# A two-block graph network: the first block's accumulators in other PSUM banks

## The chip, the cores and the metric

The kernel runs on one core of a Trainium2 chip. The metric is the device time of one execution in microseconds (us), here the median of three runs. The kernel before takes 2522.91 us (2522.33 to 2523.05).

## The reference

There are 16 graphs (`B`), each with 1024 nodes (`N`), 128 features per node and a dense 1024 x 1024 adjacency matrix, all in float32. Two residual blocks follow each other; both use the same matrix, and each ends with a layer norm over the features:

```python
# first block
degree = adj.sum(axis=-1)[:, :, None]
sum_neighbors = einsum('bid,bij->bjd', x, adj) / degree
x = layernorm(x + relu(concat([x, sum_neighbors]) @ W.T + b))
# second block: four layers; layers 2 and 3 also see earlier layers' outputs
def layer(nodes):
    src_agg = einsum('bjv,bij->biv', nodes @ ws + bs, l2norm(adj, 2))
    dst_agg = einsum('bjv,bji->biv', nodes @ wd + bd, l2norm(adj, 1))
    return tanh(concat([src_agg, nodes @ wn + bn, dst_agg]) @ wu + bu)
x = layernorm(x + layer(layer(layer(layer(x)))))
```

So each graph needs one product with its matrix in the first block, and in each of the four layers one with the column-scaled matrix and one with the row-scaled, transposed one.

## The kernel before

**Tiling.** A graph's matrix lies in SBUF as `a`: 128 partitions by 8 rows of blocks by 1024 columns. Node columns are handled in two halves of 512 (`half(h)`)[...]. Results are kept feature by node. The layers' weights are folded: `messages` (L493) makes, by eight or more products per bank `pt`, the two messages of each node, and VectorE evicts them with a bias (L506). `aggregate` (L557) multiplies them with the matrices.

**Strassen-like products.** `aggregate` splits both matrices into quarters, so that some products serve twice. The partial products M1 to M4 stand in four PSUM tiles `A`, `Bk`, `Ck` and `Dk` (three in layer 0), and two more, `Z0` and `Z1`, gather what goes into one output half alone. The upper and the lower half of the PSUM partitions are filled by two lists of products that run as pairs on the two halves of the array (L690). At fixed steps of that list, `events` read the partial products out: `m1_read`, `m4_read` and `m3_half` on ScalarE (L588 to L593, L636), `m2_read` (L596), a sum (L663) and `m3_read` (L600) on VectorE, and then `second_half`, which adds `Z1` (L604), sums (L605) and applies tanh on ScalarE (L703). `Z0` is added after the last product (L692).

**Banks.** [...]`ps_p` holds two, one for each tag p0 and p1, which `product(name, h)` gives out: `Z0` and `Z1` of every layer, and `pa` of the first block. `ps_t` holds four that rotate, under one tag: the message banks `pt`, the partial products, and `pw` of the first block (`product(name)` without a number). `ps_s` holds two for small things. A tile that is asked for gets the bank that has been given back longest, and its first product waits for the last reader of what stood there.

**Order.** The order on TensorE, VectorE, ScalarE and GpSimd is that of the program text. The main loop goes over the graphs `b`. One step of it does layers 0 to 3 of graph `b`; in between it prepares graph `n = b + 1`, by functions that `aggregate` calls at given steps of its list (`hooks`):
- in layer 0, `load(n)` issues the transfers of the next matrix `a2`; in layer 1, `sums` (L245 to L252) takes its row and column sums, on all three engines
- around layer 2, `inverses` forms the norms, and `factor_row` sends them through DRAM into a row on all partitions, `cinv`. With it `scale_columns` (L336) scales `a2` in place: 16 instructions on VectorE, the first eight for half 1 of the columns (steps 12 and 15), four for half 0 at step 19 and four at step 25, with `second_half` between these last two groups
- after layer 2, `factor_row` fetches `dinv`, into the buffer that `cinv` had, and `first_gnn` (L420) does the first block of graph `n`: for half 1 and then half 0, sixteen products (8 rows by two halves of the array) into `pa`, then VectorE multiplies by `dinv` into `agT` (L429); between the halves VectorE also combines two quarters of the matrix (L481). Then `first_weights` multiplies `x` and `agT` with the weights, in `pw`, and ScalarE applies ReLU
- in layer 3 the layer norm of graph `n` and its transposed rows follow.

The very first graph is prepared ahead of the loop by other code, so `first_gnn` runs 15 times.

Of the kernel before, what the change touches and what calls it, by code (L numbers as in the profile page):

```python
# [23 lines left out]
def adj_resnorm_kernel(ctx: ExitStack, tc: tile.TileContext, x, adj, w0, b0, layers, out):  # L24
# [46 lines left out]
    def blocks(ap):  # L71

        return ap.rearrange("p (k g c) -> p g k c", g=G, c=C)
# [5 lines left out]
    def half(h):  # L79
        return slice(h * HW, (h + 1) * HW)  # L80
# [95 lines left out]
    def by_halves(out, x, y, start=True, stop=True):  # L176

        for s in (slice(V, P), slice(V)):
            nc.tensor.matmul(out[s], x[:, s], y, start=start, stop=stop)  # L179

    def product(name, i=None):
        if i is None:
            return ps_t.tile([P, HW], F32, tag="pt", name=name)
        return ps_p.tile([P, HW], F32, tag=f"p{i}", name=name)
# [235 lines left out]
    def first_gnn(b, xn, xT, a, dinv):  # L420

        agT = one.tile([P, N], F32, tag="acc", name=f"agT{b}")
        yT = one.tile([P, N], F32, tag="x", name=f"yT{b}")
        for h in (1, 0):
            s = half(h)
            pa = product(f"pa0_{b}_{h}", h)
            for i in range(NB):
                by_halves(pa, xn[:, i], a[:, i, s], i == 0, i == NB - 1)
            nc.vector.tensor_mul(agT[:, s], pa, dinv[:, s])  # L429
            if h == 1:  # L430
                combine_1(quarters(a))
        for h in (1, 0):
            first_weights(b, h, xT, agT, yT)
        return yT
# [34 lines left out]
    def quarters(a):  # L469
        return {(j, h): a[:, j * NJ:(j + 1) * NJ, half(h)] for j in range(2) for h in range(NH)}  # L470

    def quarters_t(at):
        return {(j, h): at[h][:, j * NJ:(j + 1) * NJ] for j in range(2) for h in range(NH)}
# [5 lines left out]
    def combine_1(y):  # L479

        nc.vector.tensor_sub(y[0, 1], y[0, 1], y[0, 0])  # L481
# [75 lines left out]
    def aggregate(b, l, feats, msgs, a, at, T, Q, fT, etag, hooks={}, pieces=1):  # L557


        w = wown[l]  # L560
        n = len(feats)
        X, S = msgs
        Y = {DST: quarters(a), SRC: quarters_t(at)}
        TT = {DST: T, SRC: Q}
        low, high = slice(0, V), slice(V, P)
        Z0, Z1 = (product(f"z{h}_{l}_{b}", h) for h in range(NH))
        A, Bk, Ck = (product(f"m{i}_{l}_{b}") for i in range(3))
        e0 = one.tile([P, HW], F32, tag="e0", name=f"e0_{l}_{b}")
        e12 = one.tile([P, 2, HW], F32, tag=etag, name=f"e12_{l}_{b}")
        e1, e2 = e12[:, 0], e12[:, 1]  # L570

        def own(v, h):
            return [(w[:, c, v * V:(v + 1) * V], blocks(f[:, half(h)])) for f, c in feats]

        def src(v, h, j):
            return (X[v, j // NJ][:, j % NJ, SRC], at[h][:, j])

        def prod(name, part):
            y, t = Y[part], TT[part]
            x, y = {"M1": lambda: (X[0, 0], y[0, 0]), "M2": lambda: (S[2], t[2]), "M3": lambda: (S[3], t[3]),  # L580
                    "M4": lambda: (S[1], y[0, 1]), "Z11": lambda: (X[0, 1], y[1, 0]),
                    "Z12": lambda: (S[4], y[1, 1]), "Z21": lambda: (X[1, 1], t[4])}[name]()
            return [(x[:, k, part], y[:, k]) for k in range(NJ)]

        def m1_read():
            nc.scalar.copy(e0[high], A[high])  # L588
            nc.scalar.copy(e0[low], A[high])

        def m4_read():
            nc.scalar.copy(e2[high], Ck[low])
            nc.scalar.copy(e2[low], Ck[low])  # L593

        def m2_read():
            nc.vector.tensor_add(e0[high], e0[high], Bk[high])  # L596
            nc.scalar.copy(e1[low], e0[high])

        def m3_read():
            nc.vector.tensor_add(e0[high], e0[high], A[high])  # L600
            nc.scalar.copy(e1[high], e0[high])

        def second_half():
            nc.vector.tensor_add(e2, e2, Z1)  # L604
            nc.vector.tensor_add(e1, e1, e2)  # L605
            squash(l, 1, e1, fT)


        if l == 0:
            upper = [  # L610
                (Z1, True, own(1, 1)), (Z0, True, own(1, 0)),
                (Z1, False, [src(1, 1, j) for j in range(2, NB)]),
                (A, True, prod("M1", DST)), (Bk, True, prod("M2", DST)), (A, True, prod("M3", DST)),
                (Z0, False, prod("Z21", DST) + [src(1, 0, j) for j in range(NB)]),
            ]
            lower = [
                (Z1, True, own(0, 1)), (Z0, True, own(0, 0)),
                (Z1, False, [(S[2][:, j, SRC], at[1][:, j]) for j in range(2)] + [src(0, 1, j) for j in range(2, NB)]),
                (Ck, True, prod("M4", DST) + [src(1, 1, j) for j in range(2)]),
                (Z1, False, prod("Z12", DST)),  # L620
                (Z0, False, prod("Z11", DST) + [src(0, 0, j) for j in range(NB)]),
            ]
            def m4_and_m2_read():
                m4_read()
                m2_read()

            def m3_and_second_half():
                m3_read()
                second_half()

            events = {10: m1_read, 14: m4_and_m2_read, 18: m3_and_second_half}
        else:
            Dk = product(f"m3_{l}_{b}")

            def m3_half():
                nc.scalar.copy(e1[high], Dk[low])  # L636


            first_of_lower = [(Ck, True, prod("M4", DST) + prod("M4", SRC)), (Dk, True, prod("M3", DST))]
            reads_of_lower = [m4_read, m3_half]  # L640
            if l < NL - 1:
                first_of_lower.reverse()
                reads_of_lower.reverse()
            upper = [
                (Z1, True, own(1, 1)), (Z0, True, own(1, 0)),
                (A, True, prod("M1", DST) + prod("M1", SRC)), (Bk, True, prod("M2", DST) + prod("M2", SRC)),
                (A, True, prod("M3", SRC)),
                (Z0, False, prod("Z21", SRC) + prod("Z21", DST)),
            ]
            lower = [  # L650
                (Z1, True, own(0, 1)), (Z0, True, own(0, 0)),
                *first_of_lower,
                (Z1, False, prod("Z12", SRC) + prod("Z12", DST)),
                (Z0, False, prod("Z11", SRC) + prod("Z11", DST)),
            ]

            def first_reads():
                m1_read()
                reads_of_lower[0]()

            def m2_and_half_of_m3():
                m2_read()
                nc.vector.tensor_add(e0[high], e0[high], e1[high])  # L663

            def last_reads():
                m3_read()
                second_half()

            events = {8: first_reads, 12: reads_of_lower[1], 16: m2_and_half_of_m3, 20: last_reads}

        def steps(groups, rows):
            flat = []
            for m, (acc, first, mms) in enumerate(groups):
                later = [g[1] for g in groups[m + 1:] if g[0] is acc]
                last = not later or later[0]
                for i, (x, y) in enumerate(mms):
                    flat.append((acc[rows], x, y, first and i == 0, last and i == len(mms) - 1))
            return flat

        up, lo = steps(upper, high), steps(lower, low)  # L680
        assert len(up) == len(lo)
        for i, pair in enumerate(zip(up, lo)):
            if i - 2 * n in events:
                events[i - 2 * n]()
            if i in hooks:
                hooks[i]()
            for o, x, y, start, stop in pair:
                if len(y.shape) == 4:
                    o = nodes(o)
                nc.tensor.matmul(o, x, y, start=start, stop=stop)  # L690
        if pieces == 1:
            nc.vector.tensor_add(e0, e0, Z0)  # L692
            squash(l, 0, e0, fT)
        else:
            width = HW // pieces
            for i in range(0, HW, width):
                nc.vector.tensor_add(e0[:, i:i + width], e0[:, i:i + width], Z0[:, i:i + width])
                nc.scalar.activation(fT[:, i:i + width], e0[:, i:i + width], AF.Tanh, bias=bout[l])
# [83 lines left out]
    pa = [product(f"pa0_0_{h}", h) for h in range(NH)]  # L782
# [386 lines left out]
    b = B - 1  # L1169
# [48 lines left out]
```

## Time and profile before

| | before |
|---|---|
| time, median of 3 | 2522.91 us |
| span of the profiled run | 2517.5 us, granted clock 0.999 |
| instructions of the profiled run | 30270 |
| DMA | 219.63 MB, 87 GB/s in the mean |
| `pa` products (L179) | 960 records, 209.3 us busy |
| layer products (L690) | fourteen groups at 592 to 602 ns each |
| scaling (L336) on VectorE | 250, 683 ns in the median |
| rows `dinv`, issue to landing | 4.5 / 5.0 / 5.8 us, least, median, most |

A float32 product appears in the records as two matmuls, each with its own weight load. Two matmuls of a pair on the two halves of the array start nearly together. In the timeline each row gives the start in us, the length in us, the engine, the line, the operation, the tile written and the tiles read, the shapes and the number of records; brackets hold the idle time of that engine just before, and who ended it. PEld is the weight load of TensorE, SPq the queue that issues transfers. One step of the main loop takes some 154 us (`pa` starts at 305.44, 460.91 and 615.47 us).

### The profile page before, as it was taken

How to read it: one execution, taken by the hardware profiler on the slowest of the kernel's cores; microseconds unless marked ns; L12 is line 12 of the kernel's file. 1: busy time of each engine (PE TensorE's matmuls, PEld its weight loads, DVE VectorE, ACT ScalarE, POOL GpSimd, SP SyncE). 2: the span in 40 equal slices, each digit the busy share in tenths (PEclk: the TensorE clock that was granted, in tenths of full speed). 3: DMA queues.
4: the chain of work that ended last, by engine and by line, in shares of the span. 5: the costliest groups of instructions: out<-in, count | busy, mean ns of one | idle time of the engine just before them, and what ended most of it. 6: DMA issues, size and time to landing. Idle time of an engine off the chain costs nothing.

```text
span 2517.5 us, 30270 instructions
## 1 busy us (share of the span) xinstructions
PE 2487.2 (99%) x11693; PEld 1051.9 (42%) x11693; DVE 1661.8 (66%) x2030; ACT 836.3 (33%) x1553; POOL 519.8 (21%) x217
## 2 busy tenths in 40 slices
PE   8999999999999999999999999999999999999998
PEld 4443344433444344443434434334443344433444
DVE  5858667585665757667576675766758567585643
ACT  5414333142331423324143251432414333142311
POOL 5401204012040221302113030130301203112000
PEclk9999999999999999999999999999999999999999
DMA  9417244171543615436163351635417255271410
GB/s 207 93 45 149 54 97 103 50 143 41 101 101 69 128 34 105 103 65 126 35 125 83 83 108 46 130 67 101 95 44 147 52 97 104 49 143 42 92 24 9
DMA packets 358735, 219.63 MB, mean 87 GB/s; under 512 B 148928, under 2 KB 329408, under 8 KB 358592
## 3 DMA queue, kind: packets, MB, share of 16 engines
q1 hardware_dynamic: 357184, 213.51, 41.6%
q0 software_dynamic: 1408, 4.20, 0.7%
q8 instruction: 92, 1.51, 0.3%
q14 instruction: 51, 0.42, 0.1%
HBM read 199.17 MB, written 18.46 MB: 86 GB/s over the span
## 4 chain that ended last, share of the span: by engine, by line
PE 59%; DVE 12%; DMA 9%; SPq 7%; ACT 4%; POOL 4%; issue 2%; DVEq 0%; POOLq 0%; ACTq 0%
PE m L690 22%; PE z L690 16%; PE pt L503 10%; PE pa L179 8%; SPq L231 7%; DMA a<-in_adj_dram 4%; DVE a L336 3%; DMA cinv<-dr 2%; POOL acc L252 2%; PE pw L179 2%; DMA out_dram<-y 2%; DVE e L663 2%; POOL inv L298 1%; ACT sq L248 1%; DMA dr<-invt 1%
## 5 line engine op out<-in xcount | busy, mean ns | idle before, releaser
L378 POOL TENSOR_TENSOR rs<-ve,mhalf 128x32 f32<-128x32 f32 x30 | 162.8, 5427 | 1377.5 <-DVE ve L376 1377.5
L690 PE MATMUL m<-T,S 128*64 128x512 f32 x1008 | 395.8, 593 | 0.0
L690 PE MATMUL z<-at,t 128*64 128x512 f32 x1224 | 383.7, 592 | 0.0
L690 PE MATMUL m<-a,t 128*64 128x512 f32 x1008 | 366.7, 594 | 0.0
L690 PE MATMUL m<-Q,S 128*64 128x512 f32 x768 | 339.2, 593 | 0.0
L690 PE MATMUL m<-at,t 128*64 128x512 f32 x828 | 311.2, 592 | 0.0
L506 DVE TENSOR_TENSOR t<-pt,wm 128x512 f32<-128x512 f32 x256 | 175.2, 689 | 168.5 <-PE pt L503 168.3
L252 POOL TENSOR_TENSOR acc<-acc,sq 128x1024 f32<-128x1024 f32 x90 | 220.5, 2450 | 141.5 <-ACT sq L248 137.8
L690 PE MATMUL z<-a,S 128*64 128x512 f32 x504 | 228.3, 593 | 0.0
L690 PE MATMUL z<-a,t 128*64 128x512 f32 x504 | 226.8, 592 | 0.0
L690 PE MATMUL z<-T,t 128*64 128x512 f32 x504 | 226.8, 592 | 0.0
L336 DVE TENSOR_TENSOR a<-a,cinv 128x512 f32<-128x512 f32 x250 | 157.6, 696 | 95.8 <-DMA cinv<-dr 91.9
L179 PE MATMUL pa<-a,xn 128*64 128x512 f32 x960 | 209.3, 594 | 10.2 <-DVE e L604 10.2
L457 ACT ACTIVATE a<-a,rinv 128x256 f32<-128x256 f32 x480 | 198.2, 495 | 53.4 <-DMA a<-in_adj_dram 43.1
L503 PE MATMUL pt<-wm,f1T 128*128 128x256 f32 x768 | 213.7, 383 | 0.1
L690 PE MATMUL z<-at,S 128*64 128x512 f32 x444 | 202.6, 593 | 0.0
L690 PEld LDWEIGHTS m<-Q,S 128*64 128x64 f32 x768 | 104.1, 137 | 206.8 <-issue 206.3
L588 ACT COPY e<-m 64x512 f32<-64x512 f32 x63 | 36.6, 581 | 449.1 <-PE m L690 448.7
L690 PEld LDWEIGHTS m<-T,S 128*64 128x64 f32 x1008 | 117.8, 137 | 159.8 <-issue 158.1
L690 PE MATMUL z<-Q,t 128*64 128x512 f32 x384 | 172.6, 592 | 0.0
L690 PEld LDWEIGHTS z<-at,t 128*64 128x64 f32 x1224 | 120.7, 137 | 121.1 <-issue 111.4
L690 PEld LDWEIGHTS m<-a,t 128*64 128x64 f32 x1008 | 110.0, 137 | 125.9 <-issue 120.1
(197 smaller groups left out, 3775.5 us busy)
## 6 DMA issues: line engine op xcount, KB each, us to landing
a<-in_adj_dram SPq DMA_DIRECT2D x120, 512.0 KB, 12.5
a<-in_adj_dram SPq DMA_DIRECT2D x480, 128.0 KB, 4.1
xn<-in_x_dram SPq DMA_DIRECT2D x128, 64.0 KB, 2.0
wm<-wsave SPq DMA_DIRECT2D x16, 512.0 KB, 3.8
wm<-wsave SPq DMA_DIRECT2D x31, 256.0 KB, 2.9
xs<-in_x_dram SPq DMA_DIRECT2D x60, 128.0 KB, 3.6
cinv<-dr SPq DMA_DIRECT2D x30, 256.0 KB, 5.0
dinv<-dr SPq DMA_DIRECT2D x30, 256.0 KB, 5.0
```

The source lines that it names most:

```text
L179: nc.tensor.matmul(out[s], x[:, s], y, start=start, stop=stop)
L231: nc.sync.dma_start(ov[g, :, ks], ys[g * C:(g + 1) * C, ks])
L248: nc.scalar.activation(sq, a[:, i, :], AF.Square, accum_out=cols[:, i:i + 1])
L252: nc.gpsimd.tensor_add(acc, acc, sq)
L336: engine.tensor_mul(a[:, i, s], a[:, i, s], cinv[:, s])
L378: nc.gpsimd.tensor_tensor(rstd, ve, mhalf[:, :n], ALU.pow)
L457: nc.scalar.activation(st[:, k], st[:, k], AF.Copy, scale=rinv[:, q * QB + k:q * QB + k + 1])
L503: nc.tensor.matmul(pt[:, q], f[:, i * P:(i + 1) * P], wm[:, 1 + c], start=(k == 0), stop=(k == nch - 1))
L506: nc.vector.tensor_add(t[j][:, o:o + 2].rearrange("p k a v c -> p k (a v c)"), pt, wm[:, 0][:, None, :].to_broadcast([P, 2, 2 * P]))
L588: nc.scalar.copy(e0[high], A[high])
L663: nc.vector.tensor_add(e0[high], e0[high], e1[high])
L690: nc.tensor.matmul(o, x, y, start=start, stop=stop)
```

## The change

`first_gnn` no longer takes the banks of `Z0` and `Z1` for `pa`, but two of the rotating pool, so that its first products need not wait until the layer before has been read out of `Z1` and `Z0`. In return, `aggregate` asks for the banks of the partial products in another order: `Ck` (M4) and `Dk` (M3) first, since they are read first, then `A` and `Bk`. So the banks that come back to `pa` are those that are given back early. The order of the products, of the reads and of the transfers stays as it was.

```diff
@@ first_gnn
         for h in (1, 0):
             s = half(h)
-            pa = product(f"pa0_{b}_{h}", h)
+            pa = product(f"pa0_{b}_{h}")
             for i in range(NB):
                 by_halves(pa, xn[:, i], a[:, i, s], i == 0, i == NB - 1)
@@ aggregate
         Z0, Z1 = (product(f"z{h}_{l}_{b}", h) for h in range(NH))
-        A, Bk, Ck = (product(f"m{i}_{l}_{b}") for i in range(3))
+
+        Ck = product(f"m4_{l}_{b}")
+        Dk = product(f"m3_{l}_{b}") if l else None
+        A, Bk = (product(f"m{i}_{l}_{b}") for i in (1, 2))
@@ aggregate, layers 1 to 3
-            Dk = product(f"m3_{l}_{b}")
-
             def m3_half():
```

## The prediction

> **What bounds the kernel now.** The page first, its busy times: TensorE is the only full engine, at the full granted clock, so only time in which TensorE stands still, or does more, can move the end.
>
> ```profile
> PE 2487.2 (99%) x11693; PEld 1051.9 (42%) x11693; DVE 1661.8 (66%) x2030; ACT 836.3 (33%) x1553; POOL 519.8 (21%) x217
> PEclk9999999999999999999999999999999999999999
> ```
>
> Then the waits of TensorE alone (columns: who waited, for whom, us in total, times, longest). The reader is to see that one row holds almost half of all its idle time (10.2 of about 23 us), that the others come once or three times, and that the row is the accumulator which this change moves.
>
> ```profile
> engine line waited for: us in total, times, longest us
> PE pa L179 <- DVE e L604: 10.2, 14, 2.0
> PE w0tr L770 <- POOL inv L759: 6.3, 1, 6.3
> ```
>
> Then the timeline of one such place, all engines (start, length). It is the longest of the fifteen, in the graph step that ends layer 2 near 458 us.
>
> ```profile
> 458.36 0.59 PE L690 MATMUL z<-T,t 128*64 128x512 f32 x1
> 458.37 0.59 PE L690 MATMUL z<-a,t 128*64 128x512 f32 x1
> 458.65 0.69 DVE L663 TENSOR_TENSOR e<-e,e 64x512 f32<-64x512 f32 x1 [0.68 <-ACT e L597]
> 459.45 0.69 DVE L600 TENSOR_TENSOR e<-e,m 64x512 f32<-64x512 f32 x1
> 460.17 0.69 DVE L604 TENSOR_TENSOR e<-e,z 128x512 f32<-128x512 f32 x1
> ...
> 460.91 13.95 PE L179 MATMUL pa<-a,xn 128*64 128x512 f32 x64 [1.95 <-DVE e L604]
> ...
> 461.57 2.49 DVE L336 TENSOR_TENSOR a<-a,cinv 128x512 f32<-128x512 f32 x4
> ...
> 464.09 0.91 SPq L330 DMA_DIRECT2D dinv<-dr  x2
> ...
> 470.37 0.69 DVE L429 TENSOR_TENSOR agT<-pa,dinv 128x512 f32<-128x512 f32 x1 [5.72 <-DMA dinv<-dr]
> 470.98 2.28 DVE L481 TENSOR_TENSOR a<-a 128x2048 f32<-128x2048 f32 x1
> ...
> 474.91 0.69 DVE L429 TENSOR_TENSOR agT<-pa,dinv 128x512 f32<-128x512 f32 x1 [1.65 <-PE pa L179]
> ```
>
> TensorE finishes layer 2 and wants `pa`, half 1. Its bank is Z1's, and VectorE reads Z1 at L604 only at 460.17, because it is late: the scalings of the next graph's rows (L336) held it until 457.2, after they had waited for the row `cinv`. The chain of waits says the same: cinv's transfer, the L336 scalings, L596 to L604, then `pa`. So the bank, and nothing that `pa` computes with, starts it.
>
> [...] pairs on the two halves of the array show 0.59 us each, but a new pair starts every 0.43 us. So the idle times above are too short, and I count from start to start.
>
> **The change part by part.**
> *Removed: the wait for Z1 (and, for half 0, for L692, which had no idle time).* From the last `z` start of layer 2 to the first `pa` start, the fifteen places of the timeline show 1.36, 0.62, 2.55, 1.06, 1.14, 1.20, 1.59, 1.02, 1.56, 1.22, 1.14, 1.11, 1.35, 1.10 and 1.15 us: 19.17 in all. Undisturbed, each would be one pair's pace: 15 x 0.43 = 6.45. The stall is **12.7 us**. Cross-check: 10.2 of shown idle, plus 14 x (0.59 - 0.43) = 2.2, plus 0.2 for the one place without shown idle: 12.6.
>
> *Added: what `pa` waits for instead.* In the program as built, the banks come in the order in which they were given back: `pa` half 1 gets D's, half 0 gets C's, `pw` gets B's and A's. ScalarE copied D and C out by 446.4 in the place above, 12 us ahead. Each of the 16 row products of `pa` now has its own wait for the L336 instruction that scaled its row; before, the wait for L604 covered them. Can they bind? If `pa` starts at 458.37 + 0.43 = 458.8:
> - half 1, rows 0 to 7: scaled by 454.8, four us ahead.
> - half 0, rows 0 to 3: scaled by 457.3; rows 4 to 7 only by 464.06. Half 0 starts 16 x 0.43 = 6.9 us later, at 465.7, and comes to row 4 at 469.1: five us to spare.
> - `pw` half 1 needs agT half 1, which hangs on the row `dinv`. Its transfer is issued after the last scaling, as now, and not earlier: agT is done at 471.1. `pa` ends at 458.8 + 13.7 = 472.5, and `pw` reaches agT after its two x products, 0.86 us later, at 473.4: 2.3 us to spare.
> - `pw` half 0: VectorE runs L481 until 473.3, then the second L429 until 474.0; TensorE comes to it at 472.5 + 3 x 0.86 = 475.1. The margin is **1.1 us**, the smallest in the list, in the place with the largest gain. Where the gain is 0.7 us, it is over 2 us. Queued on VectorE behind the second L429 are the message additions (L506), which wait for TensorE anyway.
>
> *Price of the waits themselves.* `pa` has 13 more waiting products per graph: 195, and 30 `pt` products also wait for `pa`, long done. Satisfied waits cost nothing in the trace. At 109.04 the first `z<-Q` waits for nine semaphores, and it keeps the pace:
>
> ```profile
> 108.61 0.59 PE L690 MATMUL m<-Q,S 128*64 128x512 f32 x1
> 108.62 0.59 PE L690 MATMUL z<-a,S 128*64 128x512 f32 x1
> 109.04 0.59 PE L690 MATMUL z<-Q,t 128*64 128x512 f32 x1
> 109.05 0.59 PE L690 MATMUL z<-at,t 128*64 128x512 f32 x1
> ```
>
> So does a run of three waiting products at 91.88 (next pairs at 92.30 and 92.73). I take 0. The upper bound is a weight load uncovered at each: 225 x 137 ns (a 128x64 LDWEIGHTS row) = 31 us.
>
> *Moved: the order of C, D, A, B.* Within a layer each product finds a bank that the same message tile had before; apart from `pa`, `pw` and `pt` of layer 3, no instruction on any engine waits for a different one. Cost and gain: 0. The first `pt` of the next layer finds its bank read long ago in either order. Z0 and Z1 of layer 3 were waiting for agT (L429) and now for L604 and L692, both earlier: 0, since TensorE passes layer 3's messages (10.6 us) first.
>
> *Is it given back later?* The chain that made L604 late begins in layer 0 of the same graph step: the loads of the next adjacency matrix are issued at 385.93, behind a transpose (L462) that sits behind a sum from TensorE (L376, `pv`). It starts anew from TensorE's progress each time; TensorE's lead is not taken out of it. VectorE waits 168 us in all for message products: it is behind the matmuls there, not ahead of them.
>
> Sum: 2522.91 - 12.7 = **2510.2 us**.
>
> **The rivals.**
> 1. *Only the shown idle is won*: the pace from `z` to `pa` isn't kept, and 10.2 us come: 2512.7. For it: nine semaphores ahead of the first `pa`. Against: 109.04.
> 2. *The wait moves.* `pw` waits for `dinv`, or half 0 for its rows. For it: L429 waits 78.6 us in all for `dinv`, whose transfer takes 4.5 to 5.8 us and doesn't come earlier. Against: 1.1 us of margin at worst, over 2 us elsewhere. If half the stall came back there: 2516.6.
> 3. *All given back*: loads and additions late by chance elsewhere hold TensorE: 2522.9. Against: of TensorE's other waits one row repeats (`pt` behind f23T, L703), and it is 1.5 us in three times.
> 4. *Slower*: the 225 new waits each uncover a weight load: 2510.2 + 31 = 2541. For it: TensorE's weight loads run ahead of the products, which a wait could stop. Against: the two places above.
>
> **How the numbers follow.** My forecast 0.76, rival 1 0.09, rival 2 0.07, rival 3 0.05, rival 4 0.03. Faster by over 0.2% (below 2517.9): forecast, rivals 1 and 2, 0.92; same 0.05; slower 0.03. The stalls come from transfers whose landing differs by up to a microsecond, so fifteen of them vary by about 2 us in sum: 2508 to 2512.5 for the forecast; rival 1 and part of rival 2 stretch it to 2515.
>
> **What would show it.** Right: the row `pa` behind L604 is gone from TensorE's waits; the first `pa` starts 0.43 us after the last `z` start in all fifteen places; L604 now runs beside `pa`; the second L429 waits less for `pa` (31.9 us before, some 19 expected); all other TensorE waits stay as they are. Wrong: a `pa` or `pw` row behind L336, L429 or `dinv`; a pace inside `pa` above 0.43 us per pair (its 64 records longer than 13.95 us); a new `pt` wait.

## The result, and the profile after

| | before | after |
|---|---|---|
| median of 6 runs each | 2522.98 us (2522.33 to 2524.67) | 2506.06 us (2505.12 to 2506.49) |
| span of the profiled run | 2517.5 us | 2503.9 us |

The ratio is 0.9931, with a 95% interval of 0.9919 to 0.9944: 16.9 us faster, where 12.7 were forecast. 2506.06 us lies 1.9 us below 2508 us, the lower end of the stated range. So the direction and the place were right, and the size was too small; most of what follows is about those 4 us.

The waits of TensorE in the kernel after (who waited, for whom, us in total, times, longest):

```profile
PE w0tr L771 <- POOL inv L760: 6.3, 1, 6.3
PE x1tr L846 <- ACT x1n L412: 1.9, 1, 1.9
PE pt L503 <- ACT f23T L704: 1.3, 4, 0.4
PE xtr L766 <- DMA xn<-in_x_dram: 0.9, 1, 0.9
```

The first row of before, `pa` behind L604 with 10.2 us, is gone. The others are those of before within a microsecond. The timeline shows the place that the prediction walked through (start, length):

```profile
457.21 0.59 PE L691 MATMUL z<-T,t 128*64 128x512 f32 x1
457.22 0.59 PE L691 MATMUL z<-a,t 128*64 128x512 f32 x1
457.25 0.69 DVE L664 TENSOR_TENSOR e<-e,e 64x512 f32<-64x512 f32 x1 [0.68 <-ACT e L600]
457.64 13.90 PE L179 MATMUL pa<-a,xn 128*64 128x512 f32 x64
458.05 0.69 DVE L603 TENSOR_TENSOR e<-e,m 64x512 f32<-64x512 f32 x1
458.77 0.69 DVE L607 TENSOR_TENSOR e<-e,z 128x512 f32<-128x512 f32 x1
...
460.17 2.49 DVE L336 TENSOR_TENSOR a<-a,cinv 128x512 f32<-128x512 f32 x4
...
468.92 0.69 DVE L429 TENSOR_TENSOR agT<-pa,dinv 128x512 f32<-128x512 f32 x1 [5.66 <-DMA dinv<-dr]
469.53 2.28 DVE L481 TENSOR_TENSOR a<-a 128x2048 f32<-128x2048 f32 x1
471.37 1.03 PE L179 MATMUL pw<-x_T,w0T 128*64 128x512 f32 x4
471.73 0.69 DVE L429 TENSOR_TENSOR agT<-pa,dinv 128x512 f32<-128x512 f32 x1
```

`pa` starts one pair's pace (457.64 - 457.22 = 0.42 us) after the last `z`, while VectorE is still two instructions short of Z1: the read that is now L607 comes 1.1 us later and holds nobody. The row `dinv` still lands late, as foreseen, and the second L429 no longer waits for `pa` here; it ends at 472.42, ahead of the last `pw` products.

VectorE's waits and the chain that ended last say the same. First a row of the waits before, then two of after:

```profile
DVE agT L429 <- PE pa L179: 31.9, 15, 2.5
```

```profile
DVE agT L429 <- DMA dinv<-dr: 79.7, 15, 6.1
DVE agT L429 <- PE pa L179: 17.0, 14, 1.7
```

The chain, before and after:

```profile
PE 59%; DVE 12%; DMA 9%; SPq 7%; ACT 4%; POOL 4%; issue 2%; DVEq 0%; POOLq 0%; ACTq 0%
```

```profile
PE 86%; SPq 3%; DVE 2%; DMA 2%; ACT 2%; issue 2%; POOL 0%; POOLq 0%; DVEq 0%; ACTq 0%
```

L429 waits 17.0 us for `pa`, where before it was 31.9. And the chain is 86% TensorE, where before it was 59%: it no longer crosses over to transfers, scalings and L604 in each graph.

To count what no row shows, I cut TensorE's records into stages: the messages and the products of each layer, `pa` and `pw`, each from its first start to the next stage's first start. Compared with the shortest length of the same stage in any graph or profile, all of the difference lies in three stages: layer 2's products up to `pa`'s first start ("z to pa"), `pa` itself, and layer 2's messages. The rest agrees within a microsecond, apart from the start of the kernel (38.8 to 40.4 us until the first messages).

### The profile page after: what moved, and what is told of

The parts are those of the page before. It is cut to its first block, busy times and chain, and to the rows that moved or that the text cites. A ratio compares the mean times of both kernels' runs of the same rounds, so it can differ in the third digit from the quotient of the medians.

```text
span 2503.9 us, 30302 instructions
## 1 busy us (share of the span) xinstructions
PE 2484.5 (99%) x11693; PEld 1060.0 (42%) x11693; DVE 1658.2 (66%) x2030; ACT 836.3 (33%) x1553; POOL 520.8 (21%) x217
## 4 chain that ended last, share of the span: by engine, by line
PE 86%; SPq 3%; DVE 2%; DMA 2%; ACT 2%; issue 2%; POOL 0%; POOLq 0%; DVEq 0%; ACTq 0%
PE m L691 34%; PE z L691 25%; PE pt L503 15%; PE pa L179 8%; SPq L231 3%; PE pw L179 2%; DMA a<-in_adj_dram 2%; DMA out_dram<-y 1%; DVE e L664 1%; ACT sq L248 0%; ACT sq L245 0%; PE d L554 0%; DVE cols L247 0%; DVE at L462 0%; POOL acc L250 0%
## 5 line engine op out<-in xcount | busy, mean ns | idle before, releaser
L336 DVE TENSOR_TENSOR a<-a,cinv 128x512 f32<-128x512 f32 x250 | 157.7, 697 | 96.3 <-DMA cinv<-dr 92.4
```

The costliest lines, as they stand in the source:

```text
L336: engine.tensor_mul(a[:, i, s], a[:, i, s], cinv[:, s])
```

## The experiments

Two theories stood at the beginning. Both take the stall before `pa` as the cause. A says that the stall costs more than the one profile showed; B says that the change also takes time out of some other stage.

### before_again, before_third, before_fourth: the kernel before, three more profiles

The kernel is that of before, unchanged.

> The kernel before, unchanged, once more with a profile: what is open is why 16.9 us came and not 12.7. Theory A (the stall before pa is larger in most executions than in the one profile that was read, because the landing of cinv varies): about 2523 us, and the gaps from the last z to the first pa, less 0.43 us each, add up to 15 to 17 us instead of 12.7. Theory B (the stall is 12.7 us in every execution, and the change also takes idle time out of some other stage): about 2523 us with gaps adding up to 12.5 to 13 us, and some other stage of TensorE 3 to 4 us longer than in the changed kernel.

> The kernel before, a third profile of it, for the size of the stall: the first profile held 12.7 us from z to pa, the second 14.4. Theory (the first was a small sample): 13.5 to 15 us, plus 0.8 us in pa itself, and a halved clock (1.7 us) in the place near 461 us in some executions only.

> The kernel before, a fourth profile, as the third: 13.5 to 15 us from z to pa, plus 0.8 us in pa, and perhaps a halved clock near 461 us.

before_again: 2523.17 us, the median of 13 runs. The other two are single executions, of 2522.28 and 2519.05 us. With the first profile and with order_only below, whose waits are those of before, there are five profiles, and four of the changed kernel's waits:

| excess in us | z to pa | in pa | layer 2's messages | span |
|---|---|---|---|---|
| before, first profile | 13.0 | 0.8 | 4.1 | 2517.5 |
| before_again | 14.4 | 0.8 | 6.3 | 2521.2 |
| order_only | 13.9 | 2.5 | 7.6 | 2522.2 |
| before_third | 13.5 | 2.4 | 5.5 | 2520.5 |
| before_fourth | 13.0 | 0.8 | 3.5 | 2517.3 |
| after | 0.0 | 0.0 | 4.3 | 2503.9 |
| pa_only | 0.0 | 0.0 | 6.6 | 2505.6 |
| after_again | 0.0 | 0.0 | 4.3 | 2504.6 |
| after_late | 0.0 | 0.0 | 6.3 | 2505.2 |

(The forecast put 12.7 for the first profile, this count 13.0: in the seventh place the last two `z` products start 0.28 us apart, with the change too, so that 0.43 us is too much to take off there.) The mean of the first two columns is 15.0 us over the five, 13.8 in the profile that was read. Layer 2's messages vary as much in both kernels, with means of 5.4 us each, and give no difference. So B falls: no other stage is 3 to 4 us longer before. A is right that the stall costs more than 12.7 us, but not by as much as it says: before_again has 14.4 us from z to pa (15.2 with the part in `pa`), where it foresaw 15 to 17. before_fourth, with 13.0, lies 0.5 us under what was written for it. A's reason holds: in all 75 places of the five profiles the first scaling (L336), which waits for `cinv`, starts 11.07 to 11.16 us ahead of `pa`, while it starts 8.1 to 10.7 us ahead of the last `z`. The stall is as long as `cinv` is late.

In three of the five, `pa` is 0.8 us too long: 0.05 us in each of the fifteen places, 13.78 instead of 13.73 us to the first `pw`. In the other two there is a single place, near 461 us, of 15.48 us. That is in the timeline of order_only:

```profile
460.96 15.65 PE L179 MATMUL pa<-a,xn 128*64 128x512 f32 x64 [2.39 <-DVE e L607]
```

and these windows of order_only show why (columns: the stretch in us, its length, the busy time and number of PE, PEld, DVE, ACT and POOL, then the granted clock, the share of the DMA engines and GB/s):

```profile
458.00:460.90 2.90, 0.56 (x4) 0.00 (x0) 2.08 (x4) 1.23 (x2) 0.00 (x0) 1.00 0.00 0
460.90:462.00 1.10, 1.04 (x6) 0.45 (x8) 0.99 (x3) 0.27 (x1) 0.00 (x0) 0.92 0.00 0
462.00:465.00 3.00, 3.00 (x10) 0.85 (x8) 2.70 (x5) 0.72 (x2) 0.00 (x0) 0.50 0.00 0
465.00:468.00 3.00, 3.00 (x16) 1.01 (x14) 0.00 (x0) 0.46 (x1) 0.00 (x0) 0.96 0.30 73
```

TensorE has stood still for 2.4 us, and soon after it is back, the granted clock falls to 0.50 for 3.4 us; the pairs then start every 0.85 us instead of every 0.43. That costs 1.7 us. before_again has the same stall in this place, and there the clock stays:

```profile
462.00:465.00 3.00, 2.22 (x12) 0.79 (x14) 2.87 (x6) 1.34 (x2) 0.00 (x0) 1.00 0.00 0
```

### pa_only: the first part alone

```diff
-            pa = product(f"pa0_{b}_{h}", h)
+            pa = product(f"pa0_{b}_{h}")
```

> The first part of the change alone: pa in the rotating pool, A, Bk, Ck, Dk asked for in the old order. In the built program its waits are the changed kernel's, one for one. Theory (the banks of pa do everything, the order of asking nothing): the changed kernel's time, 2505 to 2507 us. Rival (the order is needed so that early banks come back to pa): between, 2510 to 2520 us, with a wait of pa on VectorE or ScalarE.

Measured: 2506.57 us (2505.80 to 2507.36), ratio 0.9932 (0.9919 to 0.9944), beside 0.9931 for the whole change. The banks of `pa` do everything.

### order_only: the second part alone

The changed kernel with `pa = product(f"pa0_{b}_{h}", h)`.

> The second part alone: C and D asked for first, pa in Z1's and Z0's banks as before. Theory (the order does nothing): the time of before, 2522 to 2524 us, and another sample of the stall before pa, 12 to 17 us in all. Rival (the 4 us beyond the forecast come from the order): 2518 to 2520 us.

Measured: 2522.39 us (2519.87 to 2523.98, 13 runs), ratio 0.9996 (0.9988 to 1.0004). The order of asking does nothing measurable, as forecast.

### half1_only: only half 1 leaves Z1

```diff
-            pa = product(f"pa0_{b}_{h}")
+            pa = product(f"pa0_{b}_{h}", None if h else 0)
```

> Only pa of half 1 leaves for the rotating pool; half 0 stays in Z0's bank, whose last reader L693 ends about a microsecond before half 0 starts. Theory (only the wait for Z1 costs): the changed kernel's time within 1 us, 2505 to 2508 us. Rival (once half 1 starts earlier, half 0 runs into the reader of Z0 in the places with the late cinv): 2508 to 2515 us and a wait of pa behind L693.

Measured: 2508.55 us (2506.38 to 2509.05), ratio 0.9938 (0.9925 to 0.9950). That is 0.6 us outside what was written. The profile decides between the theories: no gap before or in `pa`, and no wait of `pa` behind L693. Its excess lies in the messages, 7.0 us in layer 2 and 1.2 in the first layer 0. So at `pa` the wait for Z1 alone was the cost, and Z0's bank could have stayed. Why the median is 2 us above that of pa_only isn't shown.

### early_read: the same banks, but VectorE on time

```diff
-hooks = {..., 19: lambda: scale(0, 0), 25: lambda: scale(NJ, 0)}
+hooks = {..., 25: lambda: (scale(0, 0), scale(NJ, 0))}
```

> The kernel before with its banks as they were, but VectorE does the scalings of rows 0 to 3, half 0 (hook at step 19) together with those of rows 4 to 7 (step 25), so that L604 reads Z1 some 2.5 us earlier and the same work follows it. Theory (the stall is VectorE coming late to Z1's bank): the stalls of 0.2 to 2.5 us vanish, and the time is the changed kernel's, 2505 to 2509 us, with no change of banks. Rival (pa in Z1's bank costs something of its own, or half 0 now waits for its rows): 2512 us or more.

Measured: 2508.44 us (2507.27 to 2511.53), ratio 0.9942 (0.9928 to 0.9957). Its profile has no gap before `pa` and 13.73 us in it, in all fifteen places, with `pa` still in Z1's bank. So the bank itself costs nothing at `pa`: what cost was a reader that came late, and moving the reader takes the stall away as moving the bank does. The median is some 2 us above the changed kernel's; in the profile the excess lies in layer 2's messages (7.2 us), not at `pa`, and why isn't shown.

### late_two and late_read: a longer stall

```diff
 # late_two
-hooks = {..., 25: lambda: scale(NJ, 0)}
+hooks = {..., 23: lambda: scale_columns(a2, w["cinv"], range(NJ, NJ + 2), half(0)),
+         25: lambda: scale_columns(a2, w["cinv"], range(NJ + 2, NB), half(0))}
 # late_read
-hooks = {..., 25: lambda: scale(NJ, 0)}
+hooks = {..., 23: lambda: scale(NJ, 0)}
```

> The kernel before, with two of the four scalings of step 25 moved ahead of second_half, so that L604 reads Z1 1.25 us later. By idle time alone: 15 x 1.25 = 19 us more, 2542 us. If an idle time of over some 2 us also halves TensorE's granted clock for 3.4 us, as one profile showed (a loss of 1.7 us each): up to 15 x 1.7 = 26 us on top, 2542 to 2568 us, and the clock of the profile shows the halved stretches behind pa's start.

> The kernel before, with all four scalings of step 25 moved ahead of second_half: L604 reads Z1 2.5 us later. By idle time alone: 15 x 2.5 = 37 us more, 2560 us. With the clock halved behind every stall: up to 26 us on top, 2586 us.

Measured: late_two 2546.97 us (2545.51 to 2553.93), ratio 1.0102 (1.0085 to 1.0119); late_read 2578.32 us (2569.04 to 2585.07), ratio 1.0215 (1.0190 to 1.0240). The waits of TensorE in late_read:

```profile
PE pa L179 <- DVE e L604: 47.8, 15, 4.6
PE w0tr L770 <- POOL inv L759: 6.4, 1, 6.4
```

| excess in us | z to pa | in pa | places with halved clock |
|---|---|---|---|
| before (mean of five) | 13.6 | 1.4 | 2 in 75 |
| late_two | 34.1 | 5.8 | 3 in 15 |
| late_read | 50.6 | 11.7 | 7 in 15 |

From z to pa they add 20.5 and 37.0 us, as 15 x 1.25 = 19 and 15 x 2.5 = 37 would. In `pa` they add another 4.4 and 10.2 us, and in each of the places with the longer `pa` the trace has a stretch of 3.4 us at a clock of 0.5. late_read's profiled run is the fastest of its four, with a mean clock of 0.994; the others show 0.992, 0.991 and 0.988 at 2577.5, 2579.1 and 2585.1 us. So in these two profiles the longer idle times cost 4.4 and 10.2 us more than their length, and how much more differs from run to run.

### after_late: the same move in the changed kernel

The edit of late_read, in the changed kernel.

> The changed kernel with the same move as late_read: L604 comes 2.5 us later. Theory (pa no longer hangs on L604, and its rows have microseconds to spare): the changed kernel's time, 2505 to 2508 us. Rival (the bank of pw or layer 3's Z1 takes over): 2510 to 2530 us.

Measured: 2506.26 us (2505.55 to 2508.42), ratio 0.9933 (0.9918 to 0.9948). Near 457 us, where `pa` starts at 456.96, VectorE reads Z1 only 3.6 us later:

```profile
460.57 0.69 DVE L607 TENSOR_TENSOR e<-e,z 128x512 f32<-128x512 f32 x1
```

The same edit costs 55 us with `pa` in Z1's bank, and nothing with `pa` in the rotating pool. So the late read of Z1's bank is the cause of the stall.

### after_again and after_degrees: what is left in layer 2's messages

In the changed kernel, TensorE's one repeated wait is for f23T, and VectorE's row sums (L247) stand between the reads that lead to it. after_degrees does the last three of them later:

```diff
-            else:
+            elif i < NB - 3:
                 nc.vector.reduce_sum(degree, a[:, i, :], axis=AX.X)
...
         def inverses3():
             inverses(n, st)
+            degrees3((NB - 2, NB - 1))
...
+        def degrees3(rows):
+            for i in rows:
+                nc.vector.reduce_sum(st["cols"][:, 2 * NB + i:2 * NB + i + 1], a2[:, i, :], axis=AX.X)
...
-            between = {1: sums3}
+            between = {0: lambda: degrees3((NB - 3,)), 1: sums3}
```

> The changed kernel once more, beside the next one: 2505 to 2507 us, no gap before pa, and 4 to 7 us of TensorE's waiting for f23T in layer 2's messages.

> The changed kernel, with the row sums (L247) of the last three rows of blocks taken out of layer 1 and done later, one after layer 2's first message product and two after the inverses, where VectorE waits for GpSimd: so that L600 to L605, and with them f23T, are earlier. Theory (TensorE waits for f23T because these sums stand before the reads): 1 to 4 us faster than the changed kernel, 2502 to 2505 us, and the row pt behind f23T gone. Rival (f23T waits for ScalarE's squares or for the loads of the next matrix): no change, 2505 to 2507 us. Second rival (the later sums delay cinv and dinv until pw waits for them): slower, 2508 us or more.

Measured: after_again 2505.64 us (2505.34 to 2506.79), ratio 0.9941 (0.9929 to 0.9954) to a before of 2521.27 us in these runs; after_degrees 2501.14 us (2500.88 to 2501.64), ratio 0.9922 (0.9909 to 0.9936): 4.5 us faster than the changed kernel, with ranges that don't touch, and 0.9 us below what was written. TensorE's waits in after_degrees:

```profile
PE w0tr L771 <- POOL inv L760: 6.3, 1, 6.3
PE x1tr L846 <- ACT x1n L412: 1.9, 1, 1.9
PE xtr L766 <- DMA xn<-in_x_dram: 0.9, 1, 0.9
PE pt L503 <- ACT x_T L847: 0.7, 1, 0.7
```

The row behind f23T is gone, and layer 2's messages have no excess left, against 4.3 us in after_again. This version beats both kernels.

## Why the prediction was right in kind and wrong in size

- *The stall before `pa` goes, and nothing takes its place*: right. All fifteen places start at the pair's pace, and after_late shows that L604 is out of the path.
- *Margins of the new waits*: right. `pw` half 0 was the tightest, with 1.1 us forecast; in the place that the prediction walked through, its agT is ready at 472.42, and the products that need it start at 473.95, so 1.5 us were left.
- *Satisfied waits cost nothing*: right. `pa` with its 13 additional waits takes 13.73 us, less than the 13.78 of before. What rival 4 built on shows in the trace of before: the weight loads of the pair at 109.04 start at 108.61, 0.43 us ahead. Behind the unsatisfied wait at 460.91 that lead is gone: the first loads of `pa` start together with its products.
- *The order C, D, A, B: 0*: right (order_only, pa_only).
- *Nothing given back later*: right. The stages after `pw` keep their lengths within 0.1 us, and layer 2's messages vary alike in both.
- *The sum, 12.7 us* (19.17 - 6.45, under "Removed"): the step that failed. The term was too small: the stall measures 13.8 us in that same profile, and 15.0 us in the mean of five. It took the length of the stalls in one profile as what they cost in every execution, and took it off the median of other, slower executions. Four things were missing in it. In the seventh place 0.3 us was taken off too much. The second pair of `pa` starts 0.48 us after the first behind a stall, not 0.43: 0.8 us in all, since the count ended at `pa`'s first start. The longest stall, near 461 us, was followed by a halved clock in two of five profiles: 1.7 us each, so 0.7 us in the mean. And the stalls vary: 13.0 to 14.4 us, with the profile that was read at the low end; its execution took 2519.26 us, where the six timed ones took at least 2522.33. Together the five profiles give 15.0 us.
- *The range*: it allowed the stall 2 us of variation, and it took that as even on both sides of one reading, with no word on the clock.

What stays open is the difference between those 15.0 us and the 16.9 of the medians. The interval of the ratio reaches from 14.1 to 20.4 us, and in the later sets of runs pa_only, after_late and after_again were 16.9, 17.2 and 15.6 us ahead of before. The profiled executions themselves leave no rest: the five with the waits of before took 2521.5 us in the mean, the four with the changed waits 2506.6, which is 14.9 us. So the rest lies between profiled and other executions of before, which spread from 2518.55 to 2527.52 us. More halved stretches in the timed ones are not what the record shows: the granted clock is 0.9982 in the mean of 25 timed runs of before, and 0.9982 for the five profiled, while one stretch more in each would lower it by 0.0007. Whether their stalls were longer can't be told, since the timed runs have no stages.

## What to carry to other kernels

Ask of each accumulator not only how many banks there are but who reads its bank last, and what stands ahead of that reader on its engine. Here a bank elsewhere and an earlier reader both took the stall away (16.9 and 15.0 us faster). An idle time of TensorE is read from start to start and then as a lower bound: here a slower start behind it (0.05 us) and, for a long one, the clock (1.7 us) came on top. And one profile is one execution: where a stall hangs on the landing of a transfer, look at where the profiled run lies among the timed ones before taking its sum.

## What the runs showed of the hardware

The halved clock was not expected. In order_only the granted clock is 0.50 from 461.83 us for 3.41 us, and it was halved before, from 38.58 us: 423.25 us earlier, which is 124 x 3.413 us. In late_read it is halved from 39.25 us, and then 34, 80, 127, 312, 496, 543 and 589 times 3.413 us later. The profiles of before and after have no halved clock near a stall, but one in the start of the kernel, from 40.16 (to 43.57) and from 39.14 us, and one behind TensorE's last product, from 2514.82 and 2500.15 us: 725 and 721 times 3.413 us later.

By the time from the last start to the next alone, the outcome looks like chance: with 2.99 and 2.97 us order_only lost its clock and before_again did not; in before_third it was lost at 2.56 us, in late_read it was kept at 3.84 us. It looks less so when a profile is cut into stretches of 3.413 us, counted from its first halved one. These are the stretch of order_only just before its loss, the one of before_again with most of its stall, and the two of late_read that share the stall of 3.84 us (columns as above):

```profile
458.42:461.83 3.41, 1.02 (x6) 0.34 (x6) 2.89 (x5) 0.96 (x3) 0.00 (x0) 1.00 0.00 0
460.78:464.20 3.42, 1.42 (x8) 0.56 (x10) 3.18 (x6) 1.26 (x2) 0.00 (x0) 1.00 0.00 0
783.36:786.77 3.41, 1.92 (x10) 0.43 (x6) 2.93 (x5) 0.42 (x1) 0.00 (x0) 1.00 0.00 0
786.77:790.18 3.41, 1.66 (x8) 0.63 (x10) 2.92 (x5) 1.50 (x3) 0.00 (x0) 1.00 0.20 51
```

In order_only nearly the whole stall falls into one stretch, and TensorE is busy for 1.02 us of it; in the other three it is busy for 1.42 us or more, since the stall is shared between two stretches. So in these three profiles what looked like chance goes with where the stall fell. What the clock follows, and from how long a stall on it is lost, isn't shown.
